# A scan kernel with attention beside it: the side work of a step split into three places, decays moved behind the scan, chains between engines cut into links a step apart

## The chip, the cores and the metric

The kernel runs on one core of one Trainium2 chip. The metric is the device time of one execution in microseconds (us). The engines are PE (matrix products), DVE (vector), ACT (scalar functions), POOL and SP; SP issues nearly all DMAs. Each engine works through its own list of instructions in order, and semaphores order the engines among each other.

## The reference, cut to what matters

One transformer layer in fp32 on x of shape 8 x 512 x 512: a state-space (Mamba) block, cross-attention with 16 heads over a context of 512, and a mixture of 32 experts with a shared expert, each with a residual and a layernorm after it. The change lies in the part that computes the Mamba block and the attention. The core of the former is a recurrence over time for every one of 1024 channels and 16 states:

```python
dA = jnp.exp(A[None, None] * dt[..., None])
dBx = dt[..., None] * B_ssm[:, :, None, :] * x_main[..., None]
def scan_fn(h, inp):
    dA_t, dBx_t, C_t = inp
    h = dA_t * h + dBx_t
    y_t = jnp.einsum('bdn,bn->bd', h, C_t)
    return (h, y_t)
...
y = y + x_main * D_param[None, None, :]
y = y * jax.nn.silu(z)
out = res_scale * (y @ out_proj_w) + residual
```

Around it stand a layernorm of x, the input projection into x_main and z, a causal convolution with 4 taps, and the projection that gives dt, B and C.

## The kernel before, in words

`layers` computes Mamba and attention together, `experts` the routed experts, `finish` the last layernorm. Only `layers` is touched. For PE, ACT and DVE the order of instructions in `layers` is the order of the program text as it runs; DMAs on SP and work on POOL are placed by the framework.

**Steps.** Time is cut into chunks of T = 256, so there are 16 chunks (8 batches, t = 0 and t = 1). A chunk has 32 steps, k = 0 to 31: q counts four groups of two channel blocks, g four groups of four states, ci two blocks. So there are 512 steps, one scan each. A step's scan operations are, on DVE, L458 (`steps`, dtx times B into h), L462 (the scan of h with the decays l_da), L464 (the state is kept, t = 0 only) and L469 in `collect` (h times C). The decays, L446 in `decays`, are four ACT exponentials into one of two l_da tiles, made a step ahead; `carry` (L452) puts the old state into the next h tile, of which there are four. `products` (L489; L479 adds D times x at the start of a group) sums h over the states on PE into py, a step after `collect`. At k % 8 == 1 `gated` (L503) multiplies py into z.

**Side work in a step.** Between the scan and `collect` a step does its other parts: at k = 2 and 3 `back`, the output projection of the chunk before (L520), whose second half ends in `norm` (L529) and layernorm ln2; at k = 4 to 7 `gate_x`; at k % 8 == 3 `prepare`, dt by softplus (PE L398, ACT L408 to L414, DVE L418 to L421 in `both`, eight DMAs that spread dt and dtx, then `timesD` L434 on ACT); from k = 5 on what the next chunk needs: `load_x`, `norm_x` (layernorm ln1), `flip_x`, four times `convolve` (PE L311, ACT L331 and L337 in `first_tap`, DVE L345 in `other_taps`), `x_proj`.

**Attention as side units.** `units(b - 1)` is a list of closures for the attention and gating of the batch before: `flip`, `queries`, per pair of heads `maximum` (PE L783, DVE L785), `negate` (PE L792, ACT L796, DMA of nm into qa), `weigh` (PE L809, ACT L813), `gather` (PE L825; after the fourth `split`: ACT L837 writes raw, then four DMAs to attT and total), per two pairs `divide` (ACT L854 and L855, DVE L856 to L858), then `output` (PE L720, DVE L873 and L874; the last one layernorm ln3), `flip2` (PE L886), the shared expert (`hidden` L900 and L902, `shared` L914) and the router (`pick`, `choose` L563 and on, `place`). `sources(b + 1)` adds the next batch's values and keys (L691, L705). Each unit has a weight, an estimate of its PE time; a step takes units as long as the sum stays under an even share of the round of 64 steps. `work(k)` is the weight of the step's own PE work.

**Parts and their rests.** A part issues its PE work and returns a rest that reads the result. `do` runs a part and then `settle`, which runs the rests of the earlier parts; so a rest is issued behind the PE work of the next part, or at the next step's `settle`, after its scan. With `first=True` all rests are run ahead (`dry`).

Buffers that matter: two banks for dense products (tag mm), two for scores (sc), one py, and one SBUF tile shared by xp of `convolve` and l of `prepare`; xt is one tile, used by the next chunk's x and by `back`'s o.

Of the kernel before, what the change touches and what calls it, by code (L numbers as in the profile page):

```python
# [48 lines left out]
ROW = D + E + 1  # L49


def rsqrt(nc, pool, var, n, name):

    v = pool.tile([P, n], F32, tag=f"{name}v")
    nc.vector.tensor_scalar(v, var, EPS, None, ALU.add)
    r = pool.tile([P, n], F32, tag=f"{name}r")
    nc.scalar.activation(r, v, AF.Ln)
    nc.scalar.activation(r, r, AF.Exp, scale=-0.5)
    m = pool.tile([P, n], F32, tag=f"{name}m")
    nc.vector.tensor_tensor(m, v, r, ALU.mult)  # L60
    nc.vector.tensor_tensor(m, m, r, ALU.mult)
    nc.vector.tensor_scalar(m, m, -0.5, 1.5, ALU.mult, ALU.add)
    o = pool.tile([P, n], F32, tag=f"{name}o")
    nc.vector.tensor_tensor(o, r, m, ALU.mult)
    return o


def layernorm(nc, pool, tiles, outs, name):

    n = len(tiles)  # L70
    mv = pool.tile([P, n, 2], F32, tag=f"{name}mv")
    for j, t in enumerate(tiles):
        st = pool.tile([P, 6], F32, tag=f"{name}st")
        nc.vector.bn_stats(st, t)
        nc.vector.bn_aggr(mv[:, j, :], st)
    r = rsqrt(nc, pool, mv[:, :, 1], n, name)
    less = pool.tile([P, n], F32, tag=f"{name}less")
    nc.vector.scalar_tensor_tensor(less, mv[:, :, 0], -1.0, r, ALU.mult, ALU.mult)
    for j, (t, o) in enumerate(zip(tiles, outs)):
        nc.scalar.activation(o, t, AF.Identity, bias=less[:, j : j + 1], scale=r[:, j : j + 1])  # L80


def layers(ctx, tc, a, x1d, filld, based, xbuf):
# [191 lines left out]

    def load_x(b, t, f):
        f["xt"] = xt = mp.tile([P, NT_, D], F32, tag="xt", name="xt")
        nc.sync.dma_start(xt, a["x"][b, t * T : (t + 1) * T, :].rearrange("(j p) d -> p j d", p=P))  # L280

    def norm_x(f):
        xt = f["xt"]
        xs = [xt[:, j, :] for j in range(NT_)]
        layernorm(nc, sm, xs, xs, "ln1")

    def flip_x(q, f):
        if q == 0:
# [31 lines left out]
    def convolve(t, q, f):  # L320

        c0 = 2 * q
        ps = project(f, "ps_x")

        def first_tap():
            xp = mp.tile([P, 2, T + 3], F32, tag="xp", name="xp")
            if t == 0:
                nc.gpsimd.memset(xp[:, :, 0:3], 0.0)
            else:
                nc.gpsimd.tensor_copy(xp[:, :, 0:3], conv_tail[:, c0 : c0 + 2, :])  # L330
            nc.scalar.copy(xp[:, :, 3:], ps)  # L331
            if t < S // T - 1:
                nc.gpsimd.tensor_copy(conv_tail[:, c0 : c0 + 2, :], xp[:, :, T : T + 3])
            f["xs"][q] = xs = mp.tile([P, 2, T], F32, tag="xs", name="xs", bufs=5)
            for i in range(2):
                c = c0 + i
                nc.scalar.activation(  # L337
                    xs[:, i, :], xp[:, i, 0:T], AF.Identity, bias=cb[:, c : c + 1], scale=cw[:, c, 0:1]
                )

            def other_taps():
                for i in range(2):
                    acc = xs[:, i, :]
                    for k in range(1, 4):
                        nc.vector.scalar_tensor_tensor(  # L345
                            acc, xp[:, i, k : k + T], cw[:, c0 + i, k : k + 1], acc, ALU.mult, ALU.add
                        )

            return other_taps

        return first_tap

# [40 lines left out]
    def prepare(q, f):  # L393
# [8 lines left out]
        def exponentials():  # L402
# [13 lines left out]
            def both():  # L416
# [6 lines left out]
                for src in (dt, dtx):  # L423
# [2 lines left out]
                        for j in range(2):  # L426
                            nc.sync.dma_start(to[r * HP : (r + 1) * HP, :, j, :], src[j * HP : (j + 1) * HP])
                    f["ready", q].append(to)
                return lambda: timesD

            def timesD():
                for i in range(2):
# [2 lines left out]
                        f["xs"][q][:, i, :], f["xs"][q][:, i, :], AF.Identity, scale=dpar[:, c : c + 1]  # L435
                    )

            return both

        return exponentials  # L440

# [10 lines left out]
        nc.scalar.copy(h[:, :, 0:1], last if t else nothing)  # L452
        return h

    def scan(t, c, g, dtx, bc, da, h):

        steps = h.rearrange("p (j m) t -> p j m t", j=2)[:, :, :, 1:]
        nc.vector.tensor_tensor(  # L458
            steps, dtx[:, c % 2].unsqueeze(2).to_broadcast([P, 2, NG // 2, T]), bc[0], ALU.mult
        )  # L460
        flat = h.rearrange("p n t -> p (n t)")
        nc.vector.tensor_tensor_scan(flat, da.rearrange("p n t -> p (n t)"), flat, 0.0, ALU.mult, ALU.add)  # L462
        if t < S // T - 1:
            nc.vector.tensor_copy(state[:, c, g].unsqueeze(2), h[:, :, T : T + 1])  # L464
# [45 lines left out]
    def back(half, b, t, f):  # L510
# [15 lines left out]
        def norm():  # L526
            outs = [o[:, j, :] for j in range(NT_)]
            for j in range(NT_):
                nc.vector.scalar_tensor_tensor(outs[j], pos[j], rs, outs[j], ALU.mult, ALU.add)  # L529
            layernorm(nc, sm, outs, outs, "ln2")  # L530
            r0 = b * S + t * T
            nc.sync.dma_start(x1d[r0 : r0 + T, :].rearrange("(j p) d -> p j d", p=P), o)

        return norm

# [185 lines left out]
    def units(b):  # L723
# [126 lines left out]
        def divide(oc):  # L850
# [2 lines left out]
            r = p3.tile([P, D], F32, tag="row", name="r")  # L853
            nc.scalar.activation(r, total, AF.Ln)  # L854
            nc.scalar.activation(r, r, AF.Exp, scale=-1.0)  # L855
            nc.vector.tensor_tensor(total, total, r, ALU.mult)  # L856
            nc.vector.scalar_tensor_tensor(total, total, -2.0, r, ALU.add, ALU.mult)
            nc.vector.scalar_tensor_tensor(  # L858
                attT[:, oc, :], attT[:, oc, :], -1.0, total, ALU.mult, ALU.mult
            )  # L860

        def output(lt):
            if lt == 0:
# [8 lines left out]
            def add_up():  # L872
                nc.vector.tensor_tensor(xr, pp, xr, ALU.add)  # L873
                nc.vector.tensor_tensor(st["x2"][lt], xr, bo, ALU.add)  # L874
                if lt == SC - 1:
                    layernorm(nc, sm, st["x2"], st["x2"], "ln3")

            return add_up

# [81 lines left out]
                add(0, divide, (n - 3) // (2 * SC) - 1, dry=(n > pairs * SC))  # L961
        add(0, fetch, 0)
        for lt in range(SC):
            add(3.4, output, lt)
        for j in range(SC):
            add(0.5, flip2, j, dry=(j == 0))

# [40 lines left out]

    chunks = [(b, t) for b in range(B) for t in range(S // T)]
    steps = [(q, g, i) for q in range(CC // 2) for g in range(NST // NG) for i in range(2)]  # L1010
    left = []

    def settle():

        got = [part() for part in left]
        left[:] = [x for x in got if x]

    def dry():
        while left:
            settle()  # L1020

    def do(fn, *args, first=False):

        if first:
            dry()
        rest = fn(*args)
        settle()
        if rest:
            left.append(rest)

    def work(k):

        front = 6.9 if k in (2, 3) else 3.4 if 4 <= k < 8 or k in (12, 15, 18, 21, 24) else 1.0 if k in (11, 26) else 0.0
        return 1.2 + front

    f = {"xt": x0}
    norm_x(f)
    for q in range(DC // 2):
        do(flip_x, q, f)
    for q in range(CC // 2):  # L1040
# [15 lines left out]
    for i, (b, t) in enumerate(chunks):  # L1056
# [7 lines left out]
        for k, (q, g, ci) in enumerate(steps):  # L1064
            if ci == 0:
                if (q, g) != (CC // 2 - 1, NST // NG - 1):
                    bcn = bcast(f, (g + 1) % (NST // NG))
                else:
                    bcn = bcast(nf, 0) if after else None
            h = ahead  # L1070

            if k + 1 < len(steps) or after:
                nq, ng, ni = steps[(k + 1) % len(steps)]
                ahead = carry(t if k + 1 < len(steps) else after[1], 2 * nq + ni, ng)
                decays(2 * nq + ni, ng, (f if k + 1 < len(steps) else nf)["ready", nq][0], das[(n + 1) % 2])
            scan(t, 2 * q + ci, g, f["ready", q][1], bc, das[n % 2], h)
            n += 1
            if k % 8 == 1:
                if k > 1:
                    gated(q - 1, f)  # L1080
                elif old:
                    gated(CC // 2 - 1, old[2])
            if i == 0 and k == 0:
                load("Wo")
            if i == 0 and k == 2:
                biases()
            if k == 0 and old:
                twice_x(*old)
            settle()
            if k in (2, 3) and old:  # L1090
                do(back, k - 2, *old, first=True)
            if 4 <= k < 8:
                do(gate_x, k - 4, f, first=(k == 4))
            if k == 8:
                dry()
                silu(f["zs"])
            if k % 8 == 3:
                if q + 1 < CC // 2:
                    do(prepare, q + 1, f)
                elif after:  # L1100
                    do(prepare, 0, nf)
            if after:
                if k == 5:
                    load_x(*after, nf)
                if k == 9:
                    norm_x(nf)
                if k == 11:
                    for j in range(DC // 2):
                        do(flip_x, j, nf)
                if k in (12, 15, 18, 21):  # L1110
                    do(convolve, after[1], (k - 12) // 3, nf, first=(k == 12))
                if k == 23:
                    dry()
                    silu(*nf["xs"].values())
                if k == 24:
                    do(x_proj, nf)
            if side and (k >= 4 or t and k < 2):
                at = t * len(steps) + k + 1
                while side and spent + sum(own[:at]) <= whole * at / len(own):
                    w, fn, alone = side.pop(0)  # L1120
                    spent += w
                    do(fn, first=alone)

            if products:
                products()
            products = collect(2 * q + ci, g, h, bc, f)
            if ci == 1:
                bc = bcn
            while i < 2 and cleared < E * (i * len(steps) + k - 6) // (2 * len(steps) - 7):
# [363 lines left out]
```

## Time and profile before

| what | value |
|---|---|
| median of 3 runs | 5968.18 us (5965.54 to 5968.78) |
| profiled execution, its own time | 5967.24 us |
| its span | 5965.5 us |
| mean granted TensorE clock | 0.901 |
| PE, DVE, ACT, POOL busy | 84%, 75%, 42%, 8% of the span |
| scan steps | 512, first at 57.1 us, last at 4098.6 us |
| one scan, L462 | 2299 ns |

A line of the page's groups names the source line, the engine, the operation and the tiles (out<-in), then the count, the busy time, the mean duration in ns, and the idle time of the engine just before these instructions with what ended it. A line of the waits view names who waited for whom, the total in us, the times and the longest. A line of the timeline gives start and duration in us, and in brackets an idle time before it and what ended that.

### The profile page before, as it was taken

Reading aid. Unit: us, or ns where it says so; the run is one execution under the profiler, and the core shown is the slowest. Engines: PE = TensorE matmul, PEld = TensorE weight load, DVE = VectorE, ACT = ScalarE, POOL = GpSimd, SP = SyncE. Lnnn points to the kernel's source line nnn. Section 1 sums busy time; section 2 is a strip of 40 time slices with the busy share of each in tenths; the row PEclk is TensorE's granted clock in tenths of the full one; section 3 lists DMA queues with packets and bytes.
Section 4 is the critical chain, followed back from the end, with each engine's and each line's share of the span. In section 5 each row is a group of like instructions: output and inputs, shape, how many; then the busy total and the mean of one; then the engine's idle time right before and its main releaser. Section 6 shows DMA issues by size and latency. Waiting matters only on the chain. (4 is left out here: it accounts for less than half of the span.)

```text
span 5965.5 us, 60313 instructions
## 1 busy us (share of the span) xinstructions
PE 4998.5 (84%) x19752; PEld 2763.4 (46%) x19752; DVE 4468.2 (75%) x5738; ACT 2521.8 (42%) x5428; POOL 485.6 (8%) x424
## 2 busy tenths in 40 slices
PE   5658878887887888788788878878899999999995
PEld 3334334333433433343343334333367777777773
DVE  6898888888888888888888888886445556665554
ACT  4454454554445455444545544552322222222223
POOL 0000001000100100010010001001011111111111
PEclk7878989898988989898888989889999999999997
DMA  6777245333524433352443336243144445444444
GB/s 188 217 219 206 82 118 164 105 111 106 183 76 124 152 114 111 97 191 75 128 148 117 107 93 193 77 123 132 41 119 120 127 121 131 120 120 126 120 120 142
DMA packets 554282, 769.83 MB, mean 129 GB/s; under 512 B 135754, under 2 KB 268394, under 8 KB 551920
## 3 DMA queue, kind: packets, MB, share of 16 engines
q1 hardware_dynamic: 517952, 677.55, 38.2%
q0 software_dynamic: 33280, 76.90, 6.8%
q10 hardware_dynamic: 2736, 11.54, 0.5%
q8 instruction: 156, 2.56, 0.2%
q14 instruction: 158, 1.29, 0.1%
HBM read 508.68 MB, written 165.05 MB: 113 GB/s over the span
## 5 line engine op out<-in xcount | busy, mean ns | idle before, releaser
L462 DVE TENSOR_TENSOR_SCAN h<-l_da,h 128x1028 f32<-128x1028 f32 x512 | 1177.3, 2299 | 56.2 <-ACT l_da L446 14.8
L446 ACT ACTIVATE l_da<-both,l_aneg 128x256 f32<-128x256 f32 x2048 | 872.4, 498 | 444.7 <-DVE h L462 442.4
L489 PE MATMUL py<-h,l_twice 128*64 128x256 f32 x4096 | 617.8, 425 | 128.5 <-DVE h L469 128.4
L469 DVE TENSOR_TENSOR h<-h,bc 128x1024 f32<-128x1024 f32 x512 | 624.0, 1219 | 5.6
L458 DVE TENSOR_TENSOR h<-both,bc 128x1024 f32<-128x1024 f32 x512 | 623.4, 1218 | 6.4 <-DMA bc<-scr 6.4
L489 PEld LDWEIGHTS py<-h,l_twice 128*64 128x64 f32 x4096 | 288.7, 148 | 495.3 <-issue 215.2
L1242 PE MATMUL ps_h<-xT,w 128*128 128x320 f32 x1536 | 435.6, 433 | 0.0
L785 DVE TENSOR_REDUCE mx<-ps_s 128x2 f32<-128x1024 f32 x256 | 310.1, 1217 | 151.8 <-PE ps_s L783 151.6
L813 ACT ACTIVATE eT<-ps_t 128x1024 f32<-128x1024 f32 x256 | 259.9, 1018 | 348.7 <-PE ps_t L809 348.6
L809 PE MATMUL ps_t<-l_qa,l_ka 64*128 64x512 f32 x1024 | 308.4, 672 | 105.6 <-DVE mx L785 66.4
L783 PE MATMUL ps_s<-l_ka,l_qa 64*128 64x512 f32 x1024 | 318.2, 703 | 68.1 <-DVE mx L785 64.9
L1322 POOL DMA_INDIRECT based<-y,xe x160 | 251.3, 1570 | 1312.7 <-ACT y L1345 573.2
L1242 PEld LDWEIGHTS ps_h<-xT,w 128*128 128x128 f32 x1536 | 292.3, 190 | 118.2 <-issue 0.4
L1263 DVE TENSOR_TENSOR hT<-ps_h,p 128x320 f32<-128x320 f32 x128 | 62.9, 491 | 378.4 <-PE ps_h L1242 378.4
L825 PE MATMUL po<-eT,l_va 128*64 128x512 f32 x1024 | 288.9, 644 | 22.4 <-ACT raw L837 17.9
L720 PE MATMUL ps_p<-x2T,wa 128*128 128x512 f32 x512 | 286.9, 717 | 12.7 <-DVE hT L900 8.0
L1242 PE MATMUL ps_h<-t,s 128*128 128x320 f32 x1024 | 286.1, 432 | 0.0
L311 PE MATMUL ps_z<-xnT,wm 128*128 128x256 f32 x1024 | 256.2, 407 | 25.2 <-ACT dt L409 16.9
L345 DVE SCALAR_TENSOR_TENSOR xs<-xp,l_cw,xs 128x256 f32<-128x256 f32 x384 | 180.0, 482 | 108.9 <-ACT xs L337 99.2
L658 POOL DMA_INDIRECT xbuf<-x2t,dest x128 | 180.6, 1411 | 899.5 <-DVE dest L652 356.7
L311 PE MATMUL ps_x<-xnT,wm 128*128 128x256 f32 x1024 | 247.4, 396 | 0.6 <-ACT xnT L300 0.5
L311 PEld LDWEIGHTS ps_z<-xnT,wm 128*128 128x128 f32 x1024 | 202.3, 203 | 82.0 <-ACT dt L409 21.0
(231 smaller groups left out, 7471.4 us busy)
## 6 DMA issues: line engine op xcount, KB each, us to landing
bc<-scr SPq DMA_DIRECT2D x1024, 128.0 KB
w<-in_w SPq DMA_DIRECT2D x93, 1024.0 KB
wm<-in_in_proj_w SPq DMA_DIRECT2D x128, 512.0 KB
xbuf<-zero SPq DMA_DIRECT2D x32, 1362.5 KB
xe<-xbuf SPq DMA_DIRECT2D x32, 1362.5 KB
both<-dt SPq DMA_DIRECT2D x256, 128.0 KB
both<-dtx SPq DMA_DIRECT2D x256, 128.0 KB
wm<-in_out_proj_w SPq DMA_DIRECT2D x64, 512.0 KB
```

Source lines behind the costliest of these rows:

```text
L311: nc.tensor.matmul(ps[:, i, :], w[:, dc, i * P : (i + 1) * P], f["xnT"][:, dc, :], start=(dc == 0), stop=(dc == DC - 1),)
L446: nc.scalar.activation(da[:, n, 1:], dt[:, c % 2, j, :], AF.Exp, scale=aneg[:, c, j, g, m : m + 1])
L458: nc.vector.tensor_tensor(steps, dtx[:, c % 2].unsqueeze(2).to_broadcast([P, 2, NG // 2, T]), bc[0], ALU.mult)
L462: nc.vector.tensor_tensor_scan(flat, da.rearrange("p n t -> p (n t)"), flat, 0.0, ALU.mult, ALU.add)
L469: nc.vector.tensor_tensor(steps, steps, bc[1], ALU.mult)
L489: nc.tensor.matmul(py[j * HP : (j + 1) * HP, c % 2, :], twice, h[:, j * 2 + m, 1:], start=False, stop=(s == (NST // NG - 1, NG // 2 - 1, 1)),)
L720: nc.tensor.matmul(ps, lhs(dc), rhs(dc), start=(dc == 0), stop=(dc == DC - 1))
L783: nc.tensor.matmul(ps[:, j, :], qa[r, lt * P : (lt + 1) * P], ka[r, :], start=True, stop=True)
L785: return lambda: nc.vector.tensor_reduce(mx[:, lt, :].unsqueeze(2), ps, AX.X, ALU.max) and None
L809: nc.tensor.matmul(ps[:, j, :], ka[r, kc * P : (kc + 1) * P], qa[r, :], start=True, stop=True)
L825: nc.tensor.matmul(po[j * 2 * HD : (j + 1) * 2 * HD, :], va[:, kc, i, j * HD : (j + 2) * HD], eT[:, j, :], start=(kc == 0), stop=(kc == SC ...
L1242: nc.tensor.matmul(ps, w[:, n, r * P : (r + 1) * P], x[:, n, :], start=not more and n == 0, stop=n == 1, skip_group_check=more,)
```

## The change

- A step's parts are first collected in a list and then dealt over three places: behind L458 (before the scan), behind the scan and the decays, and behind `collect`. One part alone goes to the middle. Each place begins with a `settle`.
- `scan` is split: L458 becomes `steps_in`, the scan stays in `scan`. `carry` and `decays` for the next step come after the scan; before, they came ahead of L458. `products` now stands before the third place.
- A rest can be marked by `wait`: it isn't run before the next step. So marked are the norm of `back`, ln1 and ln2 between their links (statistics; Ln and Exp; the six small operations and the scaling), `other_taps`, `both` and `timesD`. ln3 has the same links without `wait`; `divide` returns its three DVE operations as a rest `newton`. `first=True` runs rests that are due, not waiting ones; before a Silu all are forced.
- `load_x` moves from k = 5 to 7, `norm_x` from 9 to 10, `flip_x` from 11 to 13, `convolve` from 12, 15, 18, 21 to 14, 16, 19, 22, its Silu from 23 to 24, `x_proj` from 24 to 25; `work` follows. The first `output` gets `dry`.

```diff
-def layernorm(nc, pool, tiles, outs, name):
+def layernorm(nc, pool, tiles, outs, name, wait=lambda part: part, then=None):
...
-    r = rsqrt(nc, pool, mv[:, :, 1], n, name)
-    less = pool.tile([P, n], F32, tag=f"{name}less")
-    nc.vector.scalar_tensor_tensor(less, mv[:, :, 0], -1.0, r, ALU.mult, ALU.mult)
-    for j, (t, o) in enumerate(zip(tiles, outs)):
-        nc.scalar.activation(o, t, AF.Identity, bias=less[:, j : j + 1], scale=r[:, j : j + 1])
+    v = pool.tile([P, n], F32, tag=f"{name}v")
+    nc.vector.tensor_scalar(v, mv[:, :, 1], EPS, None, ALU.add)
+
+    def roots():
+        r = pool.tile([P, n], F32, tag=f"{name}r")
+        nc.scalar.activation(r, v, AF.Ln)
+        nc.scalar.activation(r, r, AF.Exp, scale=-0.5)
+
+        def scaled():
+            m = pool.tile([P, n], F32, tag=f"{name}m")
+            nc.vector.tensor_tensor(m, v, r, ALU.mult)
...
+            for j, (t, o) in enumerate(zip(tiles, outs)):
+                nc.scalar.activation(o, t, AF.Identity, bias=less[:, j : j + 1], scale=r[:, j : j + 1])
+            if then:
+                then()
+
+        return wait(scaled)
+
+    return wait(roots)
...
+    left, clock = [], [0]
+
+    def wait(part):
+
+        return clock[0] + 1, part
+
+    def settle(force=False):
+
+        due, later = [], []
+        for x in left:
+            (due if force or x[0] <= clock[0] else later).append(x)
+        for _, part in due:
+            rest = part()
+            if rest:
+                later.append(rest if isinstance(rest, tuple) else (0, rest))
+        left[:] = later
+        return due
+
+    def dry(force=True):
+        while settle(force):
+            pass
...
-            return other_taps
+            return wait(other_taps)
...
-                return lambda: timesD
+                return wait(timesD)
...
-            return both
+            return wait(both)
...
-        return norm
+            return layernorm(nc, sm, outs, outs, "ln2", wait, lambda: nc.sync.dma_start(to, o))
+
+        return wait(norm)
...
     def do(fn, *args, first=False):
 
         if first:
-            dry()
+            dry(False)
...
+            thirds = [[], [], []]
+            for m, x in enumerate(parts):
+                thirds[round((m + 0.5) * 3 / len(parts) - 0.5)].append(x)
+
+            def run(m):
+                settle()
+                for x in thirds[m]:
+                    if x[0] is do:
+                        do(*x[1:-1], first=x[-1])
+                    else:
+                        x[0](*x[1:])
+
+            steps_in(2 * q + ci, h, f["ready", q][1], bc)
...
+            if k == 7 and after:
+                load_x(*after, nf)
+            run(0)
+            scan(t, 2 * q + ci, g, das[n % 2], h)
             n += 1
...
+            if k + 1 < len(steps) or after:
+                nq, ng, ni = steps[(k + 1) % len(steps)]
+                ahead = carry(t if k + 1 < len(steps) else after[1], 2 * nq + ni, ng)
+                decays(2 * nq + ni, ng, (f if k + 1 < len(steps) else nf)["ready", nq][0], das[n % 2])
+            run(1)
 
             if products:
                 products()
             products = collect(2 * q + ci, g, h, bc, f)
+            run(2)
```

## The prediction

> **What bounds the kernel now.** I began with the page: engine totals, then the slices.
>
> ```profile
> PE 4998.5 (84%) x19752; PEld 2763.4 (46%) x19752; DVE 4468.2 (75%) x5738; ACT 2521.8 (42%) x5428; POOL 485.6 (8%) x424
> ...
> PE   5658878887887888788788878878899999999995
> ...
> DVE  6898888888888888888888888886445556665554
> ...
> PEclk7878989898988989898888989889999999999997
> ```
>
> Up to slice 27 VectorE (DVE) is the fullest engine, then PE; the change lies in the first part, the 512 scan steps from 55 to 4101 us. The windows view gives DVE 3426.7 us busy there, PE 3230.0, ACT 1978.8. A step is L458, L462, (L464,) L469 on DVE, 4.8 to 5.0 us in the timeline when it holds nothing else; the mean is 4046/512 = 7.9. DVE's waits in that window, longest first:
>
> ```profile
> DVE o L529 <- PE po L520: 109.5, 30, 7.6
> DVE mx L785 <- PE ps_s L783: 107.7, 76, 4.2
> DVE xs L345 <- ACT xs L337: 85.4, 18, 8.8
> DVE dtx L418 <- ACT dtx L414: 68.2, 37, 3.4
> DVE total L856 <- ACT r L855: 46.2, 14, 6.5
> DVE zs L503 <- PE py L489: 25.0, 7, 3.6
> ```
>
> With the ten smaller rows they sum to 527 us: all that a new order of DVE's work can win here. The rest of DVE's idle time, 4046 - 3426.7 - 527 = 92 us, is gaps too short to be listed. The scan itself hardly waits: its row shows 14.8 us for l_da.
>
> The pattern repeats every 64 steps (one batch, two chunks t=0 and t=1; seven rounds carry attention). I cut one round (1491.8 to 2023.9) into stretches and asked each for its busy times and DVE waits. Columns: length, PE, PEld, DVE, ACT, POOL busy, clock.
>
> ```profile
> 1508.70:1631.10 122.40, 111.64 (x406) 57.27 (x404) 97.13 (x112) 58.92 (x135) 2.80 (x4) 0.93 0.54 166
> 1631.10:1772.40 141.30, 113.37 (x490) 43.95 (x486) 122.97 (x117) 72.35 (x146) 0.62 (x1) 0.88 0.27 74
> ...
> 1876.50:1915.70 39.20, 26.54 (x92) 12.50 (x92) 30.31 (x34) 13.92 (x34) 0.59 (x2) 0.83 0.44 107
> 1915.70:2023.90 108.20, 83.50 (x296) 41.05 (x296) 90.94 (x139) 47.19 (x103) 15.65 (x13) 0.84 0.40 117
> ```
>
> In the first stretch (A: t=0, k 2 to 17) PE is fuller than DVE and idles 10.8 us; in the others DVE is fuller. Waits: A 22.3, B (to t=1, k 1) 15.7, C (k 2 to 7) 9.0, D (k 8 to 15) 4.1, E (k 16 to 19) 8.2, F (k 20 to 31) 13.5: 72.8 a round, 510 in seven; 17 lie outside.
>
> **What the Trainium skill says.** "TensorE: Matmul & The Clock Gate", Part 1: ACT and DVE are strict FIFO. The trace agrees: a scan ends at 1937.96, its L469 could run, yet DVE stands still for 8.56 us before an L345 and reaches that L469 at 1964.65. The same page: PE's clock halves after an idle window of about 3.4 us; here L783 takes 589 to 1220 ns, so PE gaps cost twice. "VectorE: DVE Perf Modes", errata section: an fp32 tensor_tensor takes (N+151)/0.96 ns, 1224 for 1024 elements; L458 and L469 show 1218 and 1219. So moving work changes no duration. "Perfetto Trace Analysis", Most-Contended Engine: matmul busy time is a poor measure of PE's limit; so I use PE's idle time in A, not its busy share.
>
> **The change, part by part.** Instruction counts stay: layernorm's six small DVE operations and two ACT ones are the same (o becomes r), so DVE remains 3426.7 + 92. Order is what moves.
>
> *Stretch A.* At t=0, k=3, DVE ends L464 at 1516.22 and waits for back's matmuls:
>
> ```profile
> 1516.05 0.17 DVE L464 COPY l_state<-h 128x4 f32<-128x4 f32 x1
> 1523.38 0.75 DVE L529 SCALAR_TENSOR_TENSOR o<-po,l_rs,o 128x512 f32<-128x512 f32 x1 [7.16 <-PE po L520]
> 1525.10 0.75 DVE L529 SCALAR_TENSOR_TENSOR o<-po,l_rs,o 128x512 f32<-128x512 f32 x1 [0.97 <-PE po L520]
> ```
>
> The norm goes one step on, behind L469 and L458 (2.4 us): the 8.1 become 5.7, no less, because PE starts both halves (14.4 us) only after the gate L503. The 5.0 on dtx, 1.0 on m and 4.2 on xs move behind a step and go as such; zs (3.6) gains because products now come ahead of the last third's matmuls (3.7). But PE has 111.6 us of work for DVE's 97, so the saving is capped by PE's idle 10.8, which came from late evictions (ACT behind norm's chain 3.1, flips 3.0, a fetch 2.2). I take 7; ends 2 and 10.8. What is late next: PE, at the gate and at L785.
>
> *B* waits on L785 for 14.2: negate, its DMA to qa (PE idle 3.5 for it) and weigh stand close. In the new plan conv2 and a step's products (3.7 + 1.1) lie between negate0 and weigh0, and each reduction of 1.2 follows its matmul (1.0) across a scan or L469. I take 10.5; ends 5 and 14.
>
> *C* is A's case without PE's lead lost: half 1 ends some 13 us after half 0 starts, DVE arrives after about 9.4; 9.0 becomes 4.5. Ends 2 and 7. *D*: deferred both and taps; saves 3 of 4.1, ends 1 and 4.
>
> *E* gets worse. ACT's Ln waits for a DMA behind other transfers in SP's queue:
>
> ```profile
> 1877.19 0.56 ACT L837 COPY raw<-po 128x512 f32<-128x512 f32 x1
> 1886.82 0.63 ACT L854 ACTIVATE r<-total 128x512 f32<-128x512 f32 x1 [9.06 <-DMA attT<-raw]
> ```
>
> From raw to the first newton operation is 11 us, of which taps (2.96) cover a part now. The new plan puts the last gathers and divide3 in step 15; newton follows one L469 (1.2) later, with no taps before it. Behind newton stands all of step 16 on DVE, behind Ln the decays for step 17 on ACT. Raw starts up to a scan earlier, so I take a wait of 7 for 6.5, and output0's add (now behind L458 only: 3.7 - 1.2 = 2.5) and output2's (1.0) for the 1.7: 10.5 for 8.2, with rounding -3. Ends -8 and +4 (SP's order is not written by hand).
>
> *F*: ln3's four scalings reach PE so late that it idles 13.8 us, and conv3's taps wait 8.6. Now the norm falls in step 19, the flips in step 20, conv3 in 22, its taps in 23: 13.5 becomes 3. Saves 10.5; ends 6 and 13.
>
> *Costed at nothing:* the decays (4 x 498 ns and a 0.2 carry) after the scan: they have L469, L458 and the parts, 2.6 us at least, before the next scan, and their buffer's last reader is two scans back, so ACT's 442 us behind L462 mostly go; if that cover is lost, rival 3. The x1d store comes two steps later, its fetch is at k=10; load_x, which needs that tile free, moves from 5 to 7, read at 10 (15 us for 512 KB). The eight both transfers go a step later, read three steps on (15 us). POOL's three small copies per convolution queue behind taps, or behind l in the same single buffer; POOL is 8% busy. At t=0, k=19 ACT's xp copy waits for both in the next step, about 4 us, after that step's decays were issued. Side work in the tail (from 4120) is PE-bound, 0 +- 5.
>
> Sum a round: 7 + 10.5 + 4.5 + 3 - 3 + 10.5 = 32.5; seven rounds 227.5, the first and last some 5 of 17: 232. The profiled run took 5967.2 us (span 5965.5), 1.0 under the median 5968.2. 5967 - 232 = 5735. All lower ends together save 8 a round (56), all upper 53 (370): 5911 and 5597.
>
> **Rivals.**
> 1. *DVE is the bound throughout.* PE in A uses its earlier start and all short covers suffice: 56 of 72.8 go, 392 in all: 5575. For: PE idles 816 us in the loop. Against: A's 111.6 against 97.1. Chance 0.13.
> 2. *Waits only change place.* A third is 1.2 to 2.3 us, a dense product 3.7: what was evicted a whole step later (add_up, keys, shared) now waits at its third. Saves 11 a round: 5890. Against: products trail by a step, so PE may begin the next part early. 0.15.
> 3. *Slower: scans wait for decays.* Decays now stand on ACT behind evictions of the first third. By the plan some 32 of 64 steps have one. If PE can't start such a part before its step, product, eviction and decays take 3.7 + 0.6 + 1.9 = 6.2 against a bare step's 4.9: 1.3 us x 224 = 291, so 6026. It decides from 232/224 = 1.04 us a step on. Against: only eight scans wait for l_da now. 0.10.
> That the order doesn't come about is hardly possible for PE, DVE and ACT, whose order is the program's; no effect: 0.02.
>
> **Numbers.** Forecast 0.60, own range 5640 to 5830; 5735. About 0.2% (12 us) is what a measurement here can tell from no change. Faster: forecast, rival 1 and nearly all of 2, 0.87; same 0.03; slower 0.10. From 5610 to 5900 leaves out most of rival 1 and rival 3.
>
> **What would show it.** Right: loop near 3815 us with DVE still 3427 busy; L529's wait about 80, L345's and L418's under 20 each, L785's under 45; L856 about as large as now or larger; A still PE-fuller; ACT's wait on L462 under 150. Wrong: l_da ahead of L462 above 150 (rival 3), L873, L705, L914 with long waits (rival 2), or A shrunk below 108 us (rival 1).

## The result, and the profile after

The changed kernel takes 5868.81 us (median of four runs, 5851.57 to 5872.6), the kernel before 5968.4 beside it: a ratio of 0.9829, 95% interval 0.9808 to 0.9849. About 100 us are saved where 232 were forecast. The profiled execution is the fastest of the four, 5851.57 us (span 5849.9), so differences of a few us are read from the medians, not from it.

The page of the changed kernel, the rows for the engines, for two engines' slices, for the scan and for the decays:

```profile
PE 4865.5 (83%) x19752; PEld 2727.5 (47%) x19752; DVE 4459.2 (76%) x5738; ACT 2509.7 (43%) x5428; POOL 500.5 (9%) x424
...
PE   5657878787887878778787878868899999999995
...
DVE  6997988898798889879888987985356655555554
...
L491 DVE TENSOR_TENSOR_SCAN h<-l_da,h 128x1028 f32<-128x1028 f32 x512 | 1175.4, 2296 | 179.0 <-ACT l_da L472 156.2
L472 ACT ACTIVATE l_da<-both,l_aneg 128x256 f32<-128x256 f32 x2048 | 872.5, 499 | 481.4 <-DVE h L491 465.7
```

DVE is the fuller engine in most of the first 27 slices, and PE's busy time fell by 133 us without one matmul less (19752 as before; in the scan loop the mean granted clock of PE rose from 0.87 to 0.90). But the scan, which had hardly waited for its decays (14.8 us), now stands 156.2 us for them, and the decays still stand 465.7 us behind a scan. DVE's waits in the scan loop (50 to 3990 us; total, times, longest):

```profile
DVE h L491 <- ACT l_da L472: 156.2, 44, 10.4
DVE o L558 <- PE po L549: 57.1, 30, 5.0
DVE xs L371 <- ACT xs L363: 45.2, 23, 4.5
DVE total L887 <- ACT r L884: 41.6, 7, 6.5
DVE mx L814 <- PE ps_s L812: 35.6, 35, 2.4
DVE g_m L592 <- PE ps_l L585: 29.2, 7, 6.4
DVE dtx L444 <- ACT dtx L440: 25.8, 8, 3.9
```

Four of the six waits shown before have shrunk to about half or less: back's norm (L529, now L558) 109.5 to 57.1, the maximum (L785, now L814) 107.7 to 35.6, the taps (L345, now L371) 85.4 to 45.2, dtx (L418, now L444) 68.2 to 25.8. That is 207 us less; the gate (L503, now L532) fell from 25.0 to 0.6. What came instead is the first row, 141 us more than before, some 19 us at choose (L592) and 9.5 at the add behind `output` (L906, 23.1 for 13.6). The first two of these before:

```profile
DVE h L462 <- ACT l_da L446: 14.8, 8, 3.5
...
DVE g_m L563 <- PE ps_l L556: 10.7, 7, 8.1
```

One round, from scan to scan, by stretches A, B and F of the windows view (columns as before):

```profile
1479.90:1612.21 132.31, 111.04 (x423) 57.53 (x419) 102.20 (x117) 58.46 (x135) 3.67 (x4) 0.93 0.54 165
1612.21:1734.66 122.45, 106.31 (x478) 43.45 (x479) 117.77 (x114) 72.21 (x147) 0.81 (x2) 0.93 0.30 81
...
1879.49:1978.82 99.33, 78.48 (x292) 38.40 (x292) 85.59 (x127) 45.87 (x103) 16.90 (x13) 0.91 0.36 108
```

A takes 132.3 us, with PE idle for 21 of them and DVE for 30; from scan to scan it was 124.7 before. B was 139.2 and F 108.2. Some convolution work changed stretches with the steps, so I compare idle time, not length. Averages of seven rounds, worked out from the trace by adding DVE's idle gaps above 0.3 us between the scans that bound a stretch (us a round):

| stretch | before | forecast saving | after | measured saving | after, l_da alone |
|---|---|---|---|---|---|
| t=0, k 0, 1 | 0 | 0 | 1.1 | -1.1 | 1.1 |
| A (t=0, k 2-17) | 22.5 | 7 | 27.5 | -5.0 | 16.1 |
| B | 15.2 | 10.5 | 2.1 | 13.1 | 0 |
| C (t=1, k 2-7) | 9.0 | 4.5 | 1.5 | 7.5 | 0 |
| D (k 8-15) | 3.9 | 3 | 10.6 | -6.7 | 0 |
| E (k 16-19) | 7.9 | -3 | 6.0 | 1.9 | 0 |
| F (k 20-31) | 13.2 | 10.5 | 9.4 | 3.8 | 4.4 |
| sum | 71.5 | 32.5 | 58.1 | 13.4 | 21.6 |

The rows are rounded one by one.

So B and C came better than forecast. Against the forecast 12.0 us a round were lost in A, 6.7 in F, and 4.8 in D and E together (a wait moved from E into D, see below). The largest single wait of A is that of the scan of step 14 (counted from 0 as in the kernel; some expectations below call it step 15). It stands in the timeline of one round (SP, PE, ACT and DVE; an SP row is the issue of a transfer, not its landing):

```profile
1552.60 0.47 SPq L571 DMA_DIRECT2D wa<-in_Wo  x1
1555.44 2.62 SPq L453 DMA_DIRECT2D both<-dt  x4
1558.16 2.68 SPq L453 DMA_DIRECT2D both<-dtx  x4
...
1561.58 0.89 SPq L771 DMA_DIRECT2D xr<-x1d  x2
...
1555.40 0.66 PE L779 MATMUL ps_tr<-l_ident,xr 128*128 128x128 f32 x4 [2.39 <-ACT x1T L780]
1565.54 1.08 PE L779 MATMUL ps_tr<-l_ident,xr 128*128 128x128 f32 x4 [9.48 <-DVE h L498]
...
1566.66 0.59 ACT L780 COPY x1T<-ps_tr 128x512 f32<-128x512 f32 x1 [9.15 <-PE ps_tr L779]
...
1573.99 0.69 ACT L788 ACTIVATE qT<-ps_p,l_bq 128x512 f32<-128x512 f32 x1 [2.99 <-PE ps_p L749]
...
1574.66 1.70 ACT L472 ACTIVATE l_da<-both,l_aneg 128x256 f32<-128x256 f32 x4
...
1576.39 2.30 DVE L491 TENSOR_TENSOR_SCAN h<-l_da,h 128x1028 f32<-128x1028 f32 x1 [9.82 <-ACT l_da L472]
```

From the end: the scan of 1576.39 waits 9.82 us for its decays (1574.66). They stand on ACT's list behind an eviction of `queries` (1573.99), that behind the evictions of `flip` (1566.66 and one more), and these wait for PE. PE's third flip comes at 1565.54, 9.48 us after the second. In this round and one other the profile names DVE's L498 as what ended such a gap, and a transpose of x1 rows doesn't read what L498 writes; in the other five it names the rows' transfer (48.2 us in all), and I read this one so too. The rows for the third and fourth flip were issued at 1561.58, behind both's eight transfers (from 1555.44 on, 5.3 us of SP), and Wo's megabyte had been asked for at 1552.60. The same round before the change:

```profile
1588.05 2.70 SPq L427 DMA_DIRECT2D both<-dt  x4
1590.85 2.56 SPq L427 DMA_DIRECT2D both<-dtx  x4
...
1594.64 0.39 SPq L542 DMA_DIRECT2D wa<-in_Wo  x1
1599.12 0.81 SPq L742 DMA_DIRECT2D xr<-x1d  x2
```

There the eight were out before the first flip (1598.44), the rows were asked for 0.7 us after it, and PE's gap was 2.2 us.

What was the wait of E, ACT's Ln for the transfers of raw, now lies in step 15 of t=1, and so in D. The timeline, ACT:

```profile
1833.76 0.63 ACT L883 ACTIVATE r<-total 128x512 f32<-128x512 f32 x1 [7.64 <-DMA total<-raw]
```

It is 7.64 us for 9.06, and newton (L887) behind it waits 6.47 us in that round and 5.9 in the mean of the rounds, where it waited 6.0 us a round in E before.

### The profile page after: what moved, and what is told of

The parts are those of the page before. It is cut to its first block, busy times and chain, and to the rows that moved or that the text cites. A ratio compares the mean times of both kernels' runs of the same rounds, so it can differ in the third digit from the quotient of the medians.

```text
span 5849.9 us, 60211 instructions
## 1 busy us (share of the span) xinstructions
PE 4865.5 (83%) x19752; PEld 2727.5 (47%) x19752; DVE 4459.2 (76%) x5738; ACT 2509.7 (43%) x5428; POOL 500.5 (9%) x424
## 5 line engine op out<-in xcount | busy, mean ns | idle before, releaser
L491 DVE TENSOR_TENSOR_SCAN h<-l_da,h 128x1028 f32<-128x1028 f32 x512 | 1175.4, 2296 | 179.0 <-ACT l_da L472 156.2
L472 ACT ACTIVATE l_da<-both,l_aneg 128x256 f32<-128x256 f32 x2048 | 872.5, 499 | 481.4 <-DVE h L491 465.7
L498 DVE TENSOR_TENSOR h<-h,bc 128x1024 f32<-128x1024 f32 x512 | 625.9, 1223 | 12.4
L814 DVE TENSOR_REDUCE mx<-ps_s 128x2 f32<-128x1024 f32 x256 | 311.0, 1219 | 82.2 <-PE ps_s L812 79.9
L812 PE MATMUL ps_s<-l_ka,l_qa 64*128 64x512 f32 x1024 | 299.5, 661 | 18.3 <-DVE mx L814 16.1
L508 PE MATMUL py<-xs,l_ident 128*64 128x256 f32 x512 | 97.0, 454 | 209.8 <-DVE zs L532 133.2
L749 PE MATMUL ps_p<-x2T,wa 128*128 128x512 f32 x512 | 251.4, 641 | 5.5 <-ACT x2T L920 4.7
L337 PE MATMUL ps_z<-xnT,wm 128*128 128x256 f32 x1024 | 238.3, 386 | 0.0
L549 PE MATMUL po<-wm,zs 128*128 128x512 f32 x512 | 231.3, 605 | 1.9 <-DMA wm<-in_out_proj_w 1.9
```

The source lines that it names most:

```text
L337: nc.tensor.matmul(ps[:, i, :], w[:, dc, i * P : (i + 1) * P], f["xnT"][:, dc, :], start=(dc == 0), stop=(dc == DC - 1),)
L472: nc.scalar.activation(da[:, n, 1:], dt[:, c % 2, j, :], AF.Exp, scale=aneg[:, c, j, g, m : m + 1])
L498: nc.vector.tensor_tensor(steps, steps, bc[1], ALU.mult)
L812: nc.tensor.matmul(ps[:, j, :], qa[r, lt * P : (lt + 1) * P], ka[r, :], start=True, stop=True)
L814: return lambda: nc.vector.tensor_reduce(mx[:, lt, :].unsqueeze(2), ps, AX.X, ALU.max) and None
```

## The experiments

My theory after the result: the loss is the decays' new place behind evictions on ACT, made large at step 14 by late rows. Against it stood that the scans only show a wait that would fall elsewhere; that SP's transfers are late for a reason of their own; and that the three places or the links are not what gained.

**The decays ahead of the first third again** (places and links as changed):

```diff
+            if k + 1 < len(steps) or after:
+                nq, ng, ni = steps[(k + 1) % len(steps)]
+                ahead = carry(...)
+                decays(..., das[(n + 1) % 2])
             steps_in(2 * q + ci, h, f["ready", q][1], bc)
...
-            if k + 1 < len(steps) or after:
-                nq, ng, ni = steps[(k + 1) % len(steps)]
-                ahead = carry(...)
-                decays(..., das[n % 2])
             run(1)
```

> The changed kernel with carry and decays back ahead of the step's first operation; PE and DVE keep their order, only ACT's list differs. Theory 1 (ACT's list: the scans' 156 us of waiting for l_da come from decays that stand behind evictions whose product is late): l_da's wait falls under 20 us; of the 151 us in the seven rounds at least half is gained, the rest turns into waits for taps and keys: 5770 to 5800. Theory 2 (PE is simply the bound there, the wait only shows it): the wait changes its name to L371, L558 or L814 and the time stays within 15 us of 5869.

Measured 5840.15 us (5830.65 to 5853.64), ratio 0.9795 (0.9779 to 0.9811): 29 us under the changed kernel, whose interval (from 0.9808 on) it just touches, and less than the first theory asked for. PE's order is the same. DVE's waits in the loop:

```profile
DVE xs L371 <- ACT xs L363: 83.5, 23, 10.3
...
DVE h L491 <- ACT l_da L472: 53.0, 21, 5.9
```

The scan's wait fell by 103 us and the time by 29. Where PE itself is late with the rows, an early decay only lets DVE run on to the next reader of PE's work: the taps rose from 45.2 to 83.5. Order on ACT is a part of the cause, not all of it.

**Flip's rows fetched on ACT's queue:**

```diff
-                fetch(j + 1)
+                fetch(j + 1, nc.scalar)
```

> The changed kernel with the fetches of x1 rows that flip issues (three in a batch) on ACT's queue instead of SP's. Theory 1a (in SP's list these fetches stand behind the eight transfers of both, which the change puts into the same step, so PE idles 9.5 us a round, then ACT, then a scan 9.8): the wait for l_da at t=0, k=15 (70 us in seven rounds) and the 31 us for taps after it go, 5765 to 5800. Theory 2 (not SP but the two mm banks hold the flips): PE's gap before the third flip stays, time within 15 us of 5869.

Measured 5863.9 us (5855 to 5867.6), ratio 0.9823 (0.9807 to 0.9839): no change, l_da 156.1 us as before. The timeline, SP's queue, ACT's queue and PE:

```profile
1557.66 0.47 SPq L571 DMA_DIRECT2D wa<-in_Wo  x1
1560.51 2.76 SPq L453 DMA_DIRECT2D both<-dt  x4
1568.16 3.38 SPq L453 DMA_DIRECT2D both<-dtx  x4
...
1558.43 0.81 ACTq L771 DMA_DIRECT2D xr<-x1d  x2
...
1567.76 2.25 PE L779 MATMUL ps_tr<-l_ident,xr 128*128 128x128 f32 x8 [9.69 <-DMA xr<-x1d]
```

The first flip starts at 1557.47 here. The rows for the next two are asked for 1.0 us later, where the third's had been asked for 9.2 us after the first flip; still the two flips start only at 1567.76, 9.3 us after the issue, with Wo's megabyte and the first four transfers of `both` issued around them. The wait is named for the rows, so the two banks of the second theory are not what held them. One thing more than the queue changed: ACT issues in the order of the text, so the second flip's row is asked for only behind the first flip, where SP had it some 200 us ahead (1354.4 in the changed kernel). The Trainium skill ("DMA: Bandwidth & Descriptors", Issuing engines are not separate DMA queues) says that transfers of all issuing engines run on the same 16 DMA engines and interleave, so that another issuer saves only its issuing time. This agrees: SP's place was not all that held the rows. Which transfer did, this run does not show.

**No links** (a marked rest runs like any other):

```diff
-        return clock[0] + 1, part
+        return part
```

> The changed kernel without the marking: wait returns the rest itself, so every rest runs at the next settle. Theory 1: both comes a step earlier and frees SP's list before the fetches (gains up to 14 us a round), but norm, softplus and taps wait again as before (L558 and L444 some 20 us a round more): 5880 to 5930. Theory 2 (the links are what the change gains by): 5940 or slower. If the links cost by themselves: below 5850.

**All parts in the middle place:**

```diff
-                thirds[round((m + 0.5) * 3 / len(parts) - 0.5)].append(x)
+                thirds[1].append(x)
```

> The changed kernel with all parts of a step in the middle place, links kept. Theory 1: the three places give the 13 us a round that waits on L814 lost between t=0 k=18 and t=1 k=1, so these come back: 5940 to 5970. Theory 2 (the gain there came from the other placing of conv2 and negate): 5860 to 5890.

Without links 5991.09 us (5987.3 to 6001.8), ratio 1.0045 (1.0031 to 1.0059), so slower than before; with one place 5940.03 (5933.7 to 5946.7), 0.9957. DVE's waits without links:

```profile
DVE dtx L444 <- ACT dtx L440: 102.4, 39, 4.7
DVE o L558 <- PE po L549: 92.7, 30, 7.5
```

and with one place:

```profile
DVE mx L814 <- PE ps_s L812: 82.3, 57, 2.7
```

Taken out alone, the links are worth 122 us and the places 71 of what the whole change brings. Without links dtx waits 102.4 for 25.8 and the norm 92.7 for 57.1; with one place the maxima wait 82.3 for 35.6, and B's idle time is 10.4 us a round for 2.1. So the steps of the prediction that priced these (A's 5.7 for the norm, B's 10.5) had the right cause. The two numbers and the loss overlap and don't add.

**The kernel before, with the decays behind the scan:**

```diff
-                decays(..., das[(n + 1) % 2])
...
             scan(t, 2 * q + ci, g, f["ready", q][1], bc, das[n % 2], h)
+                decays(..., das[(n + 1) % 2])
```

> The kernel before with one part of the change alone: carry and decays moved behind the scan, nothing else. Theory 1 (the move puts decays behind evictions on ACT): l_da's wait, 15 us before, rises to 50 to 150, 5990 to 6060. Theory 2 (harmless, a scan has 2.6 us of cover): 5955 to 5980. If ACT's 442 us behind L462 mattered: faster than 5950.

Measured 5968.75 us, ratio 1.0002 (0.9993 to 1.0011). `carry` and the condition moved with it. No work of ACT stands between the two places there, and each engine's list is the one of the kernel before: without a first third in between the move changes nothing, not even an order.

**Split's four transfers on ACT's queue** (for newton's wait, L887):

```diff
-                nc.sync.dma_start(attT[to, oc, :], raw[r0 : r0 + HD, :])
-                nc.sync.dma_start(total[to, :], raw[r1 : r1 + HD, :])
+                nc.scalar.dma_start(attT[to, oc, :], raw[r0 : r0 + HD, :])
+                nc.scalar.dma_start(total[to, :], raw[r1 : r1 + HD, :])
```

> The changed kernel with the four transfers of split (raw to attT and total) issued from ACT behind the copy instead of from SP. Theory a (SP's list holds them behind the loads of va): L887's 5.9 and L906's 3.3 a round shrink to under 3 together, but ACT pays four issues in 64 splits: 5815 to 5850. Theory b (the transfers themselves are slow beside others): L887 stays over 4, time 5860 to 5890.

Measured 5903.05 us (5899.6 to 5904.1), ratio 0.989: 34 us slower than the changed kernel, and slower than both theories had it. L887 waits 34.9 us for 41.6, the taps, which read what ACT writes, 70.7 for 45.2. So SP's list is a small part of newton's wait. That ACT's issues are what costs the taps more is likely, but not shown apart.

**All four rows fetched in step 10** (a third xr tile, and the still unused total for the fourth row):

```diff
-            if j + 1 < SC:
-                fetch(j + 1)
...
-        add(0, fetch, 0)
+        add(0, fetch_all)
```

> The changed kernel with all four x1 tiles of a batch fetched in step 10 (three xr tiles, the fourth in the tile total, free then), so that no flip waits for a transfer; e2 had the fetches on ACT's queue, where they were issued in time but took 9 us beside the 1 MB load of Wo. Theory 1b (the flips of step 12 find their rows late because the change brings the fetches, both's eight transfers and Wo's load together): PE's 9.5 us gap goes, with it the 10 us wait of the scan of step 15 and most of the taps' 4.5: 14 a round, 5755 to 5790. Theory 2 (PE is the bound there whatever comes in time): at most 4 a round, 5840 to 5870.

**The same, with the decays ahead of the first third** (this diff and the first one together):

> e8 and e1 together: rows fetched in step 10, decays ahead of the step's first operation. Theory 1: the two losses of t=0 go, l_da's wait under 15 us in all, 5720 to 5760, which is what was forecast for the change. Theory 2: what one gives the other doesn't add, 5810 to 5845.

Rows early: 5807.27 us (5803.1 to 5816.2), ratio 0.9734 (0.9717 to 0.975), 62 us under the changed kernel. Both: 5785.08 (5783.9 to 5790.6), 0.9697 (0.9681 to 0.9713), 84 under it. Each gives less than its first theory asked for (5790 and 5760 at most). With the rows early, DVE's wait and PE:

```profile
DVE h L491 <- ACT l_da L472: 95.7, 45, 8.8
...
1545.28 1.11 PE L781 MATMUL ps_tr<-l_ident,xr 128*128 128x128 f32 x4 [0.77 <-DVE k L734]
```

DVE's waits with both:

```profile
DVE o L558 <- PE po L549: 56.6, 30, 6.9
...
DVE g_m L592 <- PE ps_l L585: 43.3, 7, 6.5
...
DVE h L491 <- ACT l_da L472: 18.4, 14, 3.6
```

With the rows there, A's wait on l_da falls from 16.1 to 6.8 us a round, and PE's gap between the second and third flip of that round is 0.77 us for 9.48; with the decays early as well l_da is 18.4 us in all, hardly more than before the change. 62 and 84: the rows are the larger part. The row of choose grew from 29.2 to 43.3: what is late next.

**A link for choose as well** (on top of the last; its scores in a bank of the score tiles, so that no dense bank is held):

```diff
-        return lambda: choose(b, x2t, pl, st)
+        last = b == B - 1
+        return (lambda: choose(b, x2t, pl, st)) if last else wait(lambda: choose(b, x2t, pl, st))
```

> The kernel with decays first and all rows fetched in step 10, and beside that one more link: `choose`, the router's sixty-odd vector operations, may run only a step after `pick`'s products (whose scores now lie in a bank of the score tiles, so that the wait keeps no bank of the dense products). If the shortfall of the last stretch (steps 20 to 31 of the second chunk) is the wait of choose on the products that stand just ahead of it (29.2 us at L592 in the changed kernel), this wait goes and the time is about 5745 us (40 below the same kernel without the link). If the products only stand behind the scores and dense products that hold PE anyway, a wait of the same size appears at a later operation (L933, L889) and the time stays at 5780 to 5790.

Measured 5756.59 us (5750.91 to 5762.37), ratio 0.9649 (0.9633 to 0.9665): 28 us under the last one where 40 were expected. This is the fastest version, 112 us under the changed kernel. DVE's waits:

```profile
DVE g_m L593 <- PE ps_l L585: 25.0, 7, 4.1
```

A step was not enough: the row (L592, here L593) is 25.0 us for 43.3, and F's idle time 6.7 us a round for 9.8. No other row took the difference over.

**Wo's load later on SP:**

```diff
         def queries(oc):
             if oc == 0:
-                load("Wo")
...
         def maximum(i, lt):
+            if (i, lt) == (0, 0):
+                load("Wo")
```

> The changed kernel, with the 1 MB load of Wo moved from the first of `queries` to the first `maximum`, some steps later; nothing else moves. If Wo's bytes, on their way at the same time, are what holds the rows that flip waits for, the scan's wait on the decays falls from 156 us to about 90 (the 9.8 us at step 15 of each round goes) and the time is about 5805. If SP is held by the eight transfers of dt and dtx ahead of the fetches, the rows come as late as before: l_da stays above 140 and the time within 5850 to 5880.

**`both` not marked to wait:**

```diff
-            return wait(both)
+            return both
```

> The changed kernel, with `both` no longer marked to wait: its four vector operations and eight transfers run at the next place instead of the next step, up to a step earlier, ahead of the fetches of `flip` or clear of them. If the transfers in the way of the fetches are the cause of the late decays at step 15, l_da falls from 156 us to about 90; against that DVE waits for ACT's softplus again (L444 from 26 to 60 or more), so the time is about 5830. If the fetches are late for another reason, l_da stays near 156, L444 rises all the same and the time is about 5900.

Neither did what it was to do. Wo later: 5873.34 us (5868.81 to 5876.03), ratio 0.9843; in the round looked at its load is still issued at 1559.67, some 3 us ahead of both's transfers and 9 ahead of the rows, for the place of a DMA on SP is not the text's. `both` at once: 5908.75 us (5900.8 to 5912.24), ratio 0.9899, 40 slower than the changed kernel; dtx waits 62.1 us again, and the order Wo, both, rows stayed on SP (1569.83, 1570.70, 1578.27), l_da 139.7. So the first says nothing on Wo; the second shows only that deferring `both` pays 40 us even with what it does to SP.

**Wo's load on ACT's queue, behind the fourth of `queries`** (ACT's order is the text's):

```diff
-        nc.sync.dma_start(w, rows(a[name]))
+        (queue or nc.sync).dma_start(w, rows(a[name]))
...
         def queries(oc):
             if oc == 0:
-                load("Wo")
...
         def maximum(i, lt):
+            if (i, lt) == (0, 0):
+                load("Wo", nc.scalar)
```

> The changed kernel, with the 1 MB load of Wo issued from ACT's queue behind the fourth of `queries`, where ACT's order keeps it some twenty us behind the rows; in the run before this one the same edit on SP's queue had left the load where it was, ahead of the rows. Theory: in the twenty us around step 15 the transfers ask for more than the queues' engines carry (the busy share stands at nine tenths), and the rows share it; with 1 MB of some 4 taken out, the rows land earlier, flip's gap on PE at step 15 shrinks from 9 us to 4 to 6, the scan's wait on the decays from 156 us to about 120, and the time is 5825 to 5850. Rival: the rows wait for the eight transfers of dt and dtx that stand ahead of them on SP's list alone; then nothing but ACT's own issue (0.5 us a round) is added, l_da stays at 150 or more and the time at 5865 to 5880.

Measured 5856.33 us (5851.54 to 5859.7), ratio 0.9812 (0.9795 to 0.9828), an interval that overlaps the changed kernel's; l_da 152.5. SP and PE:

```profile
1564.39 0.38 SPq L771 DMA_DIRECT2D xr<-x1d  x1
...
1569.09 1.08 PE L779 MATMUL ps_tr<-l_ident,xr 128*128 128x128 f32 x4 [7.32 <-DMA xr<-x1d]
```

The wait stayed where the rival had it (150 or more); the time lies between the two ranges. The third flip's row now comes in time, but the last one's is issued only at 1564.39, behind the eight transfers (1557.37 to 1563.65), though its tile was free from 1558.0 on, and PE still waits 7.32 us.

**Both at once:** the rows on ACT's queue and Wo on ACT's queue behind the fourth of `queries`.

> Both edits at once: the later fetches of `flip` on ACT's queue, and the load of Wo on ACT's queue behind the fourth of `queries`. Theory: the rows have two hindrances of which either is enough, the eight transfers ahead of them on SP's list and the megabyte that shares the transfer engines; with both gone they land 3 to 4 us after their issue, PE's gap at flip's third transpose shrinks from 9 us to under 3, the scan's wait on the decays from 156 us to 80 to 110, and the time is 5790 to 5825. Rival: the eight transfers themselves share the engines with the rows, list or no list, and only an earlier fetch helps; then the gap stays at 5 us or more, l_da at 130 or more and the time at 5840 to 5870.

Measured 5825.37 us (5818.36 to 5828.78), ratio 0.9759 (0.9743 to 0.9775): 43 us under the changed kernel, where the two edits alone gave 5 and 12. ACT's queue and PE:

```profile
1547.22 0.84 ACTq L771 DMA_DIRECT2D xr<-x1d  x2
...
1551.89 0.33 ACTq L771 DMA_DIRECT2D xr<-x1d  x1
...
1550.67 1.97 PE L779 MATMUL ps_tr<-l_ident,xr 128*128 128x128 f32 x8 [3.82 <-DVE k L734]
...
1555.23 0.63 PE L779 MATMUL ps_tr<-l_ident,xr 128*128 128x128 f32 x4 [1.05 <-DMA xr<-x1d]
```

The second and third flip start 3.5 us after their rows were asked for, where it was 9.3 with Wo beside them, and here they wait for L734, which ends at 1550.63, not for the rows. The last flip starts 3.3 us after its row was asked for, and PE has waited 1.05 us. The eight transfers of `both` go out from 1549.30 to 1554.58, so they don't hold the rows when they are not ahead of them on the list. l_da is 117.5 us, a little over the 80 to 110 expected, the time at the very end of its range. So the rows had two hindrances, eight issues ahead of them on SP and a megabyte beside them on the DMA engines, and each alone was enough to keep PE waiting (7.32 us with the first alone, 9.69 with the second). What is left of l_da is, by the runs with the decays first, ACT's order: evictions ahead of the decays.

## Why the prediction was right and wrong

**Direction, and what carries it: right.** DVE's busy time in the loop is 3417.6 us (3427 forecast); the loop itself takes 3932, where about 3815 were forecast. L529's wait was put at 80 and is 57.1, L785's under 45 and is 35.6, L856's as large as before and is 41.6 for 46.2; A is PE-fuller (111.0 to 102.2). The norm's 8.1 in A became 6.0 (forecast 5.7). Two signs failed: L345's and L418's waits, put under 20 each, are 45.2 and 25.8. B and C saved 20.6 us a round for 15 forecast. Two experiments show the causes: links 122 us, places 71.

**The step that failed: "Costed at nothing".** It put two items at nothing that were not, and the two met.

- *The decays.* "They have L469, L458 and the parts, 2.6 us at least" counts time on DVE as if ACT reached the decays at once. ACT's list is in order, and what counts is when PE ends the work of the eviction ahead. ACT's wait for the scan was to fall under 150 us and is 465.7. It stands for 145 waits in which ACT, 43% busy, was early and waited for the scan that frees a tile, which costs nothing; 44 times ACT was late and DVE waited. That is rival 3's mechanism, and its mark (above 150) was reached at 156.2; but 156.2 over the 224 steps that it counts is 0.70 us a step, under the 1.04 from which it decides, so it ate the gain in A and took from F without turning the sign.
- *The transfers.* "The eight both transfers go a step later, read three steps on" looks at who reads them. What counted was who is issued behind them: the rows of `flip`. I had followed the first fetch only ("at k=10"); the later ones are issued as the flips free their tiles, into both's and Wo's transfers.

So A, put at +7 us a round, came out at -5.0. With rows and decays early (the run of 5785.08 us) it is +5.7: 16.8 us of idle time for 22.5. That it comes so close to 7 is in part luck: the waits on dtx, m and zs went or nearly went as said, but the taps' 4.2, which was to go too, is 4.5 after the change and 4.7 in that run, and the keys wait 2.6 there. The two items are worth 84 of the 134 us between forecast and result.

**F, +10.5 forecast, +3.8 measured.** I followed ln3 and conv3 and left out `choose`, 10.7 us in the profile before. It now reads its scores right behind their products, which stand behind a dense product: 4.2 us a round, and 6.2 once the decays no longer wait. A link for it gave 28 us. The scan of one step (t=1, k=25) waits the other 4.4 for its decays; with the decays first about 0.4 us a round are left.

**D and E** together were to change nothing and lost 4.8. Newton's own wait was right (7 forecast, 5.9 measured, in step 15); larger or new are the maxima in D (2.8 for 1.2) and dtx in E (3.4). What these two come from was not tested.

**Rivals.** Rival 1 did not come: 58.1 of 71.5 us a round remain. Rival 2's price, 11 us a round, is near the measured 13.4, but its cause isn't what was seen: of the evictions that it named, L906 (before L873) went from 13.6 us to 23.1, and L734 and L947 wait 2.0 or less. Rival 3 above.

With the two items and `choose` mended the kernel takes 5756.59 us; 5735 was forecast. The 22 us left are not traced further; the taps' wait in A, 4.8 us a round there, is the largest that was to go and did not.

## What to carry to other kernels

When work is moved on an engine that other engines feed, list for each in-order queue, transfer queues too, what now stands ahead of the item that the critical engine reads next, and ask when that can be done; cover counted on the reader's side alone is not cover. A deferred group of transfers has to be checked against what is issued behind it, not only against its own reader. And when a removed wait gives less than its size, look for the next reader of the same late producer before giving up the cause: two hindrances that each suffice show little when taken away one at a time (5 and 12 us here, and 43 together).

## What was not expected of the hardware

- Rows of 256 KB, two of them issued together on a queue of their own, reached PE 9.3 us after their issue (1558.43 to 1567.76) with a megabyte issued 0.8 us ahead of them and four transfers of 128 KB behind them; with the megabyte gone two such rows took 3.5 us at most (1547.22 to 1550.67), and one 3.3 us (1551.89 to 1555.23).
- Issuing eight transfers held SP 5.2 to 6.7 us in the rounds looked at, longer than the 3.3 us of a row. The skill's section named above calls the issuing time usually small beside the transfer. For one transfer this agrees (0.66 us, an eighth of 5.3); the sum of eight on one list is what counted here.
- After PE's gap of 9.48 us four transposes took 1.08 us; the four before it 0.66. The granted clock was 1.00 from 1552 to 1556 and 0.50 from 1558 to 1570, so a part of each such gap is paid again behind it.
